# Layer 3's value product in three float32r passes over the key tiles, with its result turned through DRAM

## The chip, the cores and the metric

The kernel runs on one core of one Trainium2 chip. The metric is device time in microseconds of one execution. A run's time is a little longer than the span that the profile covers, which goes from the first to the last instruction of the core.

## What is computed

Input `x` has 32 batches of 512 tokens with 128 features; `adj` is one 512 × 512 matrix that all batches share. Four layers follow one another, each of the form `x = x + layer(relu(layernorm(x)), adj)`. The change is in the last one:

```python
# layer 3, h = relu(layernorm(x))
Q = x @ q
K = x @ k
A = jnp.einsum('bnd,bmd->bnm', Q, K)
A = A / jnp.sqrt(jnp.float32(input_dimension))
A = jnp.tanh(A / 8.0) * 8.0
A = jnp.exp(A) * A_shape
A = A / jnp.sum(A, axis=-1, keepdims=True)
out = A @ x @ v          # x is h here, A_shape is adj
```

All of it is float32. The kernel computes `A @ (h @ v)`, and calls `h @ v` of a batch `hv`. Layers 0 to 2 are graph layers of other kinds; only the end of layer 2 touches the change.

## The kernel before

**Tiles.** A batch of 512 tokens is held as four blocks of 128 tokens on the partitions (token-major), or with the 128 features on the partitions and the 512 tokens along the row (feature-major). [...] A product can be made in float32, which the profile shows as two instructions for each 128 columns, or as a sum of three products in float32r: both operands are split beforehand into parts called high, low and mid (`three`, and the helpers `moving_parts`, `fixed_parts`, `scaled_parts`, `bank_parts` at L420 to L445), so that the three passes together give the exact product up to a known factor, `UP`.

**Turning.** Token-major h becomes feature-major in two steps (`turn_half`, L1144): VectorE transposes 32 × 32 blocks (L1150), and four writes to a DRAM tile followed by one read (`fetch`, L1159) move the blocks to their places. The tokens then lie in a permuted order, which the reading patterns called `crossed` and `split` undo.

**Layer 3, batch by batch.** For each batch n:

- `key_parts(n)` splits feature-major h into three key parts: ScalarE (L437), VectorE (L438), GpSimd (L439).
- `queries(n)` multiplies the parts with the product of q and k (L1271), and splits the result, the query, by ScalarE and VectorE (L443 to L445).
- `mapped(n)` makes hv: a float32 product of the four 128-token blocks of h with v (`projected`, L458), eight instructions in all, copied by VectorE from PSUM into an SBUF tile with a 129th column of ones (L1282, L1283). That column later gives the row sums.
- `scores(n)` makes the 512 × 512 scores in four tiles of three passes (L1298). ScalarE takes tanh (L1299) and exp (L1291); then the mask is multiplied in, by VectorE for tiles 0 and 2 and by GpSimd for 1 and 3 (L1293).
- `attended(n)` multiplies with hv in float32 (L1320), and VectorE divides by the row sum and adds to x (L1322, L1324). The batch is then written out.

**Order.** The order on TensorE, VectorE, ScalarE and GpSimd is that of the source, written out by hand in `layers_2_and_3` (from L1340); DMAs that are wrapped in `keep_in_program_order` keep theirs in SP's queue. The loop of layer 3 is shifted by stages: turn n does `queries(n+1)`, `key_parts(n+2)`, `scores(n)`, `attended(n-1)` and `mapped(n+1)`, with the turning of later batches between. The last two batches are written out apart. The loop of layer 2 ahead of it does per turn `opened(n+1)` (L1212, L1215), `summed(n)` (L1235), `weighed_by_phi(n+1)` (p_z, L458) and `updated(n-1)` (p_l, L458); its last turns already make the key parts of batches 0 and 1 and the query of batch 0.

**Buffers that matter.** All products take one of eight PSUM banks in rotation. `small_tile` gives one of 13 buffers (query parts, hv, and in layer 2 the parts of h, features and hidden rows). `matrix_tile` gives one of three larger ones; in layer 3 the mask holds one of them.

Of the kernel before, what the change touches and what calls it, by code (L numbers as in the profile page):

```python
# [9 lines left out]
F32 = mybir.dt.float32  # L10
F32R = mybir.dt.float32r
# [3 lines left out]
OP = mybir.AluOpType  # L15
AX = mybir.AxisListType

P = 128
QR = 32
NQR = P // QR  # L20
# [3 lines left out]
LOW = 4096.0  # L24
DOWN = 1.0 - 1.0 / 8192.0
UP = 1.0 + 1.0 / 4096.0
# [3 lines left out]
def kernel(  # L30
# [37 lines left out]
    nc = tc.nc  # L68
    B, N, D = x.shape
    NT = N // P  # L70
# [11 lines left out]
    bounce = ctx.enter_context(tc.tile_pool(name="bounce", bufs=4, space=bass.MemoryType.DRAM))  # L82

    def bank(name):
        return psum.tile([P, 512], F32, tag="bank", name=name)
# [11 lines left out]
    def matrix_tile(name, dtype=F32):  # L97
        return const.tile([P, NT, N], dtype, tag="matrix", name=name, bufs=3)
# [4 lines left out]
    def small_tile(name, dtype=F32):  # L103
        return after.tile([P, N], dtype, tag="small", name=name, bufs=13)
# [72 lines left out]
    vw = load_rows(v_w, "vw")[:, 0, :]  # L177
# [244 lines left out]
    def moving_parts(x, high, low, mid):  # L422

        nc.scalar.activation(high, x, AF.Copy, scale=DOWN)  # L424
        nc.gpsimd.tensor_sub(low, x, high.bitcast(F32))  # L425
        nc.vector.scalar_tensor_tensor(mid, x, 1.0 / UP, high.bitcast(F32), OP.mult, OP.subtract)
# [26 lines left out]
    def projected(name, *terms):  # L453

        p = bank(name)
        for t in range(NT):
            for i, (hT, w) in enumerate(terms):
                nc.tensor.matmul(p[:, blk(t)], hT(t), w, start=(i == 0),  # L458
                                 stop=(i == len(terms) - 1))
        return tiles(p)  # L460
# [78 lines left out]
    for t in range(NT):  # L539
        for s in range(t + 1):  # L540
            nc.tensor.matmul(pi[:, t : t + 1], upto[:, s, blk(t)], rch[:, s : s + 1],
                             start=(s == 0), stop=(s == t))

    p = bank("p_qk_t")
# [27 lines left out]
    parts = []  # L572
# [9 lines left out]
    hT = {q: feature_major(f"hT0_{q}") for q in range(4)}  # L582
# [5 lines left out]
    for t in range(NT):  # L588
# [4 lines left out]
        for j in range(NT):  # L593
            nc.tensor.matmul(pg[j // 2][:, j % 2, :], m[:, t, blk(j)], of_row[:, t, :],
                             start=(t == 0 and j % 2 == 0), stop=(t == NT - 1), skip_group_check=True)
    pb = bank("p_known")[:, : 2 * NK].rearrange("p (k e) -> p k e", e=2)
    for kk in range(NK):
        for t in range(NT):
            nc.tensor.matmul(pb[:, kk, :], of_row[:, t, blk(kk)], known[:, t, :],
                             start=(t == 0), stop=(t == NT - 1))  # L600
# [565 lines left out]
    def hT_of(layer, n):  # L1166
        return hTs[layer, n // 2][:, :, n % 2, :]
# [3 lines left out]
    keys, query, hvs, exs = {}, {}, {}, {}  # L1171
# [47 lines left out]
    def weighed_by_phi(n):  # L1219

        if n >= B:
            return
        p = projected(f"p_z_{n}", (columns(features[n]), w2[:, 0, :])).rearrange("p t f -> p (t f)")
        if n:
            z = matrix_tile(f"z_{n}", F32R)
            weighed_features[n] = [z[:, i] for i in range(3)]
        else:
            weighed_features[n] = three(f"z_{n}")
        bank_parts(p, *weighed_features[n])
# [8 lines left out]
    def relu_of(n):  # L1238

        hidden[n] = small_tile(f"hidden_{n}")  # L1240
        nc.scalar.activation(crossed(hidden[n]), split(sums2[n]), AF.Relu, bias=phi1b, scale=UP)
# [15 lines left out]
    def key_parts(n):  # L1257

        if n >= B:
            return  # L1260
        both = wide_tile(f"key_{n}", F32R)
        keys[n] = [both[:, i].rearrange("p (t n) -> p t n", t=NQR) for i in range(3)]
        scaled_parts(hT_of(3, n), *keys[n])

    def queries(n):

        if n >= B:
            return
        p = bank(f"p_query_{n}")
        for i in range(3):  # L1270
            nc.tensor.matmul(p, qk_parts[i], keys[n][i], start=(i == 0), stop=(i == 2))  # L1271
        query[n] = three(f"query_{n}")
        bank_parts(p, *query[n])

    def mapped(n):

        if n >= B:
            return
        hT = hT_of(3, n)
        p = projected(f"p_hv_{n}", (lambda t: hT[:, t, :], vw))  # L1280
        hv = hvs[n] = after.tile([P, NT, D + 1], F32, tag="small", name=f"hv_{n}", bufs=13)
        nc.vector.memset(hv[:, :, D : D + 1], 1.0)  # L1282
        nc.vector.tensor_copy(hv[:, :, :D], p)  # L1283

    def scores(n):

        ex = exs[n] = wide_tile(f"ex_{n}")
        mask = adjTx[0]

        def exponential(t):  # L1290
            nc.scalar.activation(ex[:, t, :], ex[:, t, :], AF.Exp, scale=8.0)  # L1291
            eng = nc.gpsimd if t % 2 else nc.vector
            eng.tensor_mul(split(ex[:, t, :]), split(ex[:, t, :]), crossed(mask[:, t, :]))  # L1293

        for t in range(NT):
            p = bank(f"p_score_{n}_{t}")
            for i in range(3):
                nc.tensor.matmul(p, keys[n][i][:, t, :], query[n][i], start=(i == 0), stop=(i == 2))  # L1298
            nc.scalar.activation(crossed(ex[:, t, :]), split(p), AF.Tanh, scale=UP / (8.0 * math.sqrt(D)))  # L1299
            if t:  # L1300
                exponential(t - 1)
        exponential(NT - 1)
# [25 lines left out]
        if width > 1 and end == NT:  # L1328
            tc.keep_in_program_order(nc.sync.dma_start(out_r, x))

    qk_parts = []

    def weights_of_3():

        parts = small_tile("qk_parts", F32R)[:, : 3 * D].rearrange("p (i f) -> p i f", f=D)
        qk_parts.extend(parts[:, i, :] for i in range(3))
        moving_parts(qk, *qk_parts)
        nc.gpsimd.tensor_scalar(vw, vw, 1.0 / LOW, 1.0, OP.mult, OP.mult)

    def layers_2_and_3():  # L1340


        later, ready, rooted = iter(range(B)), [(2, 6)], []
        late_stats = [stats_steps(q) for q in range(NQ - 4, NQ)]
        stats_of_3 = [stats_steps(q, low=True) for q in range(NQ - 1)]

        def ahead_of_3():
            m = next(later, B)
            if m < B:
                chunk(3, m)  # L1350
                ready.append((3, m))

        def turn_ready(now):
            for layer, m in now:
                turn_half(layer, m)

        mask_of = adjT_d.rearrange("(a b c) w -> b a c w", a=NT, c=QR)
        for n in range(B):
            opened(n + 1)
            turn_ready(ready)  # L1360
            ready = []
            for steps in rooted:
                next(steps)
            if 7 <= n < B - 1:
                ahead_of_3()
            if n + 7 < B:
                chunk(2, n + 7)
                ready.append((2, n + 7))
            split_hT(n + 2)
            for steps in rooted:  # L1370
                go(steps)
            rooted = []
            halves = [(stats_of_3, n - 2)] if 2 <= n else []
            halves += [(late_stats, n)] if n < 8 else []
            for of_pair, m in halves:
                go(of_pair[m // 2], 2)
                if m % 2:
                    rooted.append(of_pair[m // 2])
            summed(n)
            biased(n)  # L1380
            relu_of(n)
            if n == B - 1:
                queries(0)
            weighed_by_phi(n + 1)
            updated(n - 1)
            if n == 0:
                fetch(2, 2)
            elif n % 2 and n + 5 < B:
                fetch(2, n // 2 + 3)
            if n == 12:  # L1390
                weights_of_3()
            if n == 20:
                adjTx.append(matrix_tile("adjTx"))
            if n >= 20 and n % 2 and n < 28:
                i = (n - 20) // 2
                tc.keep_in_program_order(nc.sync.dma_start(adjTx[0][:, i, :], mask_of[i]))
            if n in (26, 28, 30):
                fetch(3, (n - 26) // 2)
            if n in (29, 30):
                key_parts(n - 29)  # L1400
        for steps in rooted:
            go(steps)
        last_stats = low_stats(NQ - 1)
        key_parts(2)
        mapped(0)
        updated(B - 1)
        for n in range(B):
            last = n == B - 1
            queries(n + 1)
            if n:  # L1410
                key_parts(n + 2)
            if n in (4, 6, 8):
                go(last_stats, 1)
            if last:
                attended(n - 2, NT // 2)
            else:
                scores(n)
                if n == B - 2:
                    attended(n - 1, 0, NT // 2)
                    mapped(n + 1)  # L1420
                    scores(n + 1)
                    continue
            attended(n - 1)
            mapped(n + 1)
            if n % 2:
                turn_ready(ready)
                ready = []
            elif n:
                ahead_of_3()
            if n % 2 == 0:  # L1430
                fetch(3, n // 2 + 3)
        attended(B - 1, width=1)
# [109 lines left out]
```

## Time and profile before

| what | value |
|---|---|
| runs | 889.18, 890.08, 890.42 us; median 890.08 |
| the profiled execution | 888.95 us |
| its span | 887.2 us, 15609 instructions |
| TensorE clock granted | 1.00 |
| layer 3's loop | from about 630 us to the end |
| products p_hv (L458) | 256 instructions, first 628.8, last 871.6 us |
| copies to hv (L1283), VectorE | 32 of 684 ns |
| masks (L1293) | VectorE 64 of 1268 ns, GpSimd 64 of 1559 ns |
| HBM | read 44.11 MB, written 40.89 MB |

Durations are of one instruction. A TensorE product starts before the one ahead of it has ended, so its duration (275 ns for p_hv) is longer than its distance from the next; the chain of work counts the distance. PE is TensorE, PEld its loading of weights, DVE VectorE, ACT ScalarE, POOL GpSimd, SPq the queue of SyncE, which issues nearly all DMAs.

### The profile page before, as it was taken

What the parts mean: (1) busy time and instruction counts of PE and PEld (TensorE: products, weight loads), DVE (VectorE), ACT (ScalarE), POOL (GpSimd) and SP (SyncE); (2) the same over time, 40 slices, a digit from 0 to 9 for tenths busy, and PEclk for the clock granted to TensorE, in tenths of its full rate; (3) what the DMA queues carried; (4) which work ended last, traced back from release to release, by engine and by line L of the source; (5) the groups of instructions that cost most, each with busy time, mean ns of one, the idle gap of its engine ahead of it and who ended that gap; (6) DMA issues with size and microseconds to landing.
All of it is one profiled execution on the core that took longest, in us unless ns stands there. A gap on an engine that the chain in (4) does not pass through costs nothing.

```text
span 887.2 us, 15609 instructions
## 1 busy us (share of the span) xinstructions
PE 879.2 (99%) x5369; PEld 774.3 (87%) x5369; DVE 712.5 (80%) x1476; ACT 569.8 (64%) x1288; POOL 598.8 (67%) x535
## 2 busy tenths in 40 slices
PE   8999999999999999999999999999999999999998
PEld 4899999988888888888888888888899999999997
DVE  7888887568787887888688887787799888887775
ACT  5874454456656556556666888876677677766664
POOL 5876999976767877767586665663565666556652
PEclk9999999999999999999999999999999999999999
DMA  9166554032313122222242444555113223322111
GB/s 266 44 170 167 166 144 114 29 96 71 117 51 96 48 72 72 59 85 72 72 143 72 117 125 139 146 157 149 48 60 100 71 69 107 85 82 62 48 37 48
DMA packets 83919, 86.02 MB, mean 97 GB/s; under 512 B 6912, under 2 KB 74624, under 8 KB 83840
## 3 DMA queue, kind: packets, MB, share of 16 engines
q1 hardware_dynamic: 83552, 84.50, 33.6%
q8 instruction: 42, 0.69, 0.3%
q10 hardware_dynamic: 288, 0.52, 0.2%
q14 instruction: 37, 0.30, 0.1%
HBM read 44.11 MB, written 40.89 MB: 96 GB/s over the span
## 4 chain that ended last, share of the span: by engine, by line
PE 95%; POOL 2%; ACT 1%; issue 1%; DMA 1%; DVE 0%; SPq 0%; POOLq 0%; ACTq 0%
PE p_av L1320 13%; PE p_l L1031 10%; PE p_hidden L1235 10%; PE p_score L1298 10%; PE p_x1T L409 9%; PE p_w L1010 5%; PE p_l_c L397 4%; PE p_hv L458 3%; PE p_z L458 3%; PE p_l_a L397 3%; PE p_l L458 3%; PE p_l_d L397 3%; PE p_g L458 3%; PE p_w L1012 3%; PE p_query L1271 3%; PE p_feat L1212 3%
## 5 line engine op out<-in xcount | busy, mean ns | idle before, releaser
L1320 PEld LDWEIGHTS p_av<-hv,ex 128*128 128x128 f32 x1024 | 119.3, 191 | 2.8
L439 POOL TENSOR_TENSOR key<-key 128x512 fp32r<-128x512 f32 x32 | 49.5, 1547 | 104.4 <-DVE key L438 53.5
L1320 PE MATMUL p_av<-hv,ex 128*128 128x129 f32 x1024 | 119.5, 274 | 0.0
L289 ACT ACTIVATE h<-x,sh,rs 128x128 f32<-128x128 f32 x256 | 102.1, 483 | 12.0 <-DVE sh L259 11.0
L1293 DVE TENSOR_TENSOR ex<-ex,adjTx 128x512 f32<-128x512 f32 x64 | 81.2, 1268 | 33.6 <-ACT ex L1291 31.9
L1293 POOL TENSOR_TENSOR ex<-ex,adjTx 128x512 f32<-128x512 f32 x64 | 98.6, 1559 | 10.4 <-ACT ex L1291 6.2
L1141 ACT ACTIVATE h<-x,sh,rs 128x128 f32<-128x128 f32 x256 | 102.9, 486 | 0.0
L247 DVE BATCH_NORM_STATS2 bn<-x 128x6 f32<-128x256 f32 x244 | 87.3, 418 | 0.0
L425 POOL TENSOR_TENSOR low_h<-h,high_h 128x512 fp32r<-128x512 f32 x32 | 54.5, 1706 | 46.1 <-PE p_w L1012 28.0
L1291 ACT ACTIVATE ex<-ex 128x512 f32<-128x512 f32 x128 | 78.8, 650 | 0.0
L1299 ACT ACTIVATE ex<-p_score 128x512 f32<-128x512 f32 x128 | 73.8, 603 | 1.4 <-PE p_score L1298 1.1
L443 ACT ACTIVATE high_query<-p_query 128x512 fp32r<-128x512 f32 x32 | 19.2, 599 | 70.0 <-PE p_query L1271 70.0
L1199 POOL TENSOR_SCALAR high_hT<-hT 128x512 fp32r<-128x512 f32 x32 | 20.1, 629 | 56.5 <-PE p_hidden L1215 31.8
L1255 POOL TENSOR_TENSOR x<-x,phi2b 128x256 f32<-128x256 f32 x64 | 56.6, 905 | 0.0
L425 POOL TENSOR_TENSOR low_hs<-hs,high_hs 128x512 fp32r<-128x512 f32 x32 | 44.4, 1398 | 13.0 <-ACT high_hs L424 12.7
L411 ACT COPY x1T<-p_x1T 128x512 f32<-128x512 f32 x32 | 18.7, 585 | 52.2 <-PE p_x1T L409 52.2
L1298 PE MATMUL p_score<-high_query,key 128*128 128x512 f32 x128 | 50.5, 395 | 0.0
L1298 PE MATMUL p_score<-low_query,key 128*128 128x512 f32 x128 | 50.5, 394 | 0.0
L1298 PE MATMUL p_score<-mid_query,key 128*128 128x512 f32 x128 | 50.4, 394 | 0.0
L256 ACT ACTIVATE sd<-bn,eps 128x8 f32<-128x8 f32 x46 | 13.9, 303 | 55.0 <-DVE bn L247 50.9
L1012 PE MATMUL p_w<-th,x1T 128*128 128x128 f32 x256 | 49.0, 273 | 0.0
L444 DVE SCALAR_TENSOR_TENSOR z<-p_z,z 128x512 fp32r<-128x512 f32 x31 | 21.4, 691 | 32.7 <-ACT z L443 32.6
(253 smaller groups left out, 2631.4 us busy)
## 6 DMA issues: line engine op xcount, KB each, us to landing
d<-hb SPq DMA_DIRECT2D x128, 128.0 KB, 2.4
hT<-d SPq DMA_DIRECT2D x32, 512.0 KB, 3.8
d_hT<-hb_hT SPq DMA_DIRECT2D x112, 128.0 KB, 2.4
hT<-d_hT SPq DMA_DIRECT2D x28, 512.0 KB, 3.4
x<-in_x_dram SPq DMA_DIRECT2D x32, 256.0 KB, 4.7
out_dram<-x SPq DMA_DIRECT2D x31, 256.0 KB, 2.3
adjT_d<-adj_squares SPq DMA_DIRECT2D x4, 256.0 KB, 4.6
adj_crossed<-in_adj_dram SPq DMA_DIRECT2D x4, 256.0 KB
```

Of the source, the lines that this page charges most:

```text
L247: nc.vector.bn_stats(st[:, k].rearrange("p e s -> p (e s)"), xt[q][:, b, t : t + 2, :].rearrange("p t f -> p f t"))
L289: nc.scalar.activation(h[:, b, t, :], xt[q][:, b, t, :], AF.Relu, bias=shift[q][:, i : i + 1], scale=scale[q][:, i : i + 1])
L397: nc.tensor.matmul(p[:, i * 2 * D : (i + 1) * 2 * D], a[:, k, blk(i)], b[:, k], start=(first and i == 0 and k == 0), stop=(k == 1), skip_g ...
L409: nc.tensor.matmul(p, right[part][:, blk(t)], left[part][:, t, :], start=(t == 0 and part == 0), stop=(t == NT - 1 and part == 2))
L425: nc.gpsimd.tensor_sub(low, x, high.bitcast(F32))
L458: nc.tensor.matmul(p[:, blk(t)], hT(t), w, start=(i == 0), stop=(i == len(terms) - 1))
L1031: nc.tensor.matmul(p, adj_parts[part][:, t, blk(i)], w[r][part][:, t, :], start=(part == 0 and t == 0), stop=(part == 2 and t == NT - 1))
L1141: nc.scalar.activation(h[:, t, :], xt[q][:, b, t, :], AF.Relu, bias=shift[q][:, i : i + 1], scale=scale[q][:, i : i + 1])
L1235: nc.tensor.matmul(sums2[n], weighed_features[n][i][:, blk(t)], sq[i][:, t, :], start=False, stop=(i == 2 and t == NT - 1), skip_group_che ...
L1293: eng.tensor_mul(split(ex[:, t, :]), split(ex[:, t, :]), crossed(mask[:, t, :]))
L1298: nc.tensor.matmul(p, keys[n][i][:, t, :], query[n][i], start=(i == 0), stop=(i == 2))
L1320: nc.tensor.matmul(po[:, i, : D + 1], ex[:, t, blk(i0 + i)], hv[:, t, :], start=(t == 0), stop=(t == NT - 1))
```

## The change

`mapped(n)` no longer multiplies token blocks of h with v. It multiplies v, split once into three float32r parts (`vw_parts`), with the three key parts of the batch, which are feature-major h already split: three passes of 512 columns. The result lies feature-major in PSUM. VectorE transposes its 32 × 32 blocks into a small tile, four DMAs write them to a DRAM tile, and one reads them back into a matrix tile (`hvt`). A new function, `straight_values(n)`, has GpSimd copy that tile in straight order into the hv tile, beside a column of `1.0 / UP` that GpSimd sets.

The places in the order change as well. `mapped(0)` and `mapped(1)` are issued in the last two turns of layer 2's loop; `mapped(n+1)` stands ahead of the scores of batch n, right behind the next query; `straight_values(n)` stands behind the scores of n, and for batch 0 ahead of them. `weights_of_3` splits v in place of scaling it by `1.0 / LOW`.

```diff
+    values, turned_values = {}, {}
+
     def mapped(n):
 
         if n >= B:
             return
-        hT = hT_of(3, n)
-        p = projected(f"p_hv_{n}", (lambda t: hT[:, t, :], vw))
+        p = bank(f"p_hv_{n}")
+        for i in range(3):
+            nc.tensor.matmul(p, vw_parts[i], keys[n][i], start=(i == 0), stop=(i == 2))
+        hb = small_tile(f"hvb_{n}").rearrange("p (j t r) -> p j t r", j=NQR, t=NT)
+        nc.vector.transpose(hb.rearrange("p j t r -> p t j r"), p.rearrange("p (t j c) -> p t j c", t=NT, c=QR))
+        d = bounce.tile([NQR, QR, NQR, P], F32, tag="dv", name=f"dv_{n}", bufs=4)
+        for i in range(NQR):
+            tc.keep_in_program_order(
+                nc.sync.dma_start(d[:, :, i, :].rearrange("j c e -> c j e"),
+                                  hb[i * QR : (i + 1) * QR].rearrange("c j t r -> c j (t r)")))
+        raw = turned_values[n] = matrix_tile(f"hvt_{n}")[:, 0]
+        tc.keep_in_program_order(
+            nc.sync.dma_start(raw, d.rearrange("j c i e -> (j c) (i e)")))
+
+    def straight_values(n):
+
+        if n >= B:
+            return
         hv = hvs[n] = after.tile([P, NT, D + 1], F32, tag="small", name=f"hv_{n}", bufs=13)
-        nc.vector.memset(hv[:, :, D : D + 1], 1.0)
-        nc.vector.tensor_copy(hv[:, :, :D], p)
+        nc.gpsimd.memset(hv[:, :, D : D + 1], 1.0 / UP)
+        nc.gpsimd.tensor_copy(hv[:, :, :D].rearrange("p t (i r) -> p t i r", r=QR),
+                              turned_values[n].rearrange("p (i t r) -> p t i r", i=NQR, t=NT))
...
-    qk_parts = []
+    qk_parts, vw_parts = [], []
...
         moving_parts(qk, *qk_parts)
-        nc.gpsimd.tensor_scalar(vw, vw, 1.0 / LOW, 1.0, OP.mult, OP.mult)
+        parts = small_tile("vw_parts", F32R)[:, : 3 * D].rearrange("p (i f) -> p i f", f=D)
+        vw_parts.extend(parts[:, i, :] for i in range(3))
+        moving_parts(vw, *vw_parts)
...
             relu_of(n)
+            if n == B - 2:
+                mapped(0)
             if n == B - 1:
                 queries(0)
+                mapped(1)
             weighed_by_phi(n + 1)
...
         key_parts(2)
-        mapped(0)
         updated(B - 1)
         for n in range(B):
             last = n == B - 1
             queries(n + 1)
             if n:
+                mapped(n + 1)
                 key_parts(n + 2)
...
             else:
+                if n == 0:
+                    straight_values(0)
                 scores(n)
+                if n:
+                    straight_values(n)
                 if n == B - 2:
                     attended(n - 1, 0, NT // 2)
-                    mapped(n + 1)
                     scores(n + 1)
+                    straight_values(n + 1)
                     continue
             attended(n - 1)
-            mapped(n + 1)
```

## The prediction, made before the result was known

> **What bounds the kernel now.** I read the page's busy shares first, then the chain that ended last, then a table of busy time by stage, then the order of time inside layer 3. The page says TensorE is busy for 99% of the span, and the chain is 95% TensorE:
>
> ```profile
> PE 879.2 (99%) x5369; PEld 774.3 (87%) x5369; DVE 712.5 (80%) x1476; ACT 569.8 (64%) x1288; POOL 598.8 (67%) x535
> ...
> PE 95%; POOL 2%; ACT 1%; issue 1%; DMA 1%; DVE 0%; SPq 0%; POOLq 0%; ACTq 0%
> ```
>
> An average says nothing of one stage, so here are two stretches of layer 3 (window, us, then busy us and instructions by engine):
>
> ```profile
> 660.00:700.00 40.00, 40.00 (x278) 36.65 (x277) 36.53 (x73) 30.48 (x63) 23.82 (x18) 1.00 0.25 74
> 820.00:870.00 50.00, 50.00 (x346) 45.76 (x345) 38.50 (x81) 32.98 (x66) 28.33 (x18) 1.00 0.15 46
> ```
>
> TensorE never idles in either; asked for the waits of TensorE between 640 and 870 us, the trace lists none. VectorE is second, 36.53 of 40 us at worst. The chain's pieces (start, duration, what) give one turn of layer 3's loop:
>
> ```profile
> 642.40 0.89 PE p_hv L458 x8
> 643.30 0.69 PE p_query L1271 x3
> 643.99 2.78 PE p_score L1298 x12
> 646.77 3.57 PE p_av L1320 x32
> 650.34 0.89 PE p_hv L458 x8
> ```
>
> One turn is 650.34 − 642.40 = 7.94 us, all TensorE. p_hv costs 0.89 us in eight instructions, a three-pass product of 512 columns (p_query) 0.69 to 0.70. So what the change takes off TensorE comes off the end, unless something else becomes late.
>
> [...] an fp32 product of 128 columns costs 0.89 / 4 = 0.22 us, as much as one pass of 512 columns (2.79 / 12 = 0.23). [...] L1293 on VectorE takes 0.69 us with GpSimd idle and 1.67 beside it; L1324, which reads PSUM, stays at 0.35 to 0.36 beside it:
>
> ```profile
> 742.11 0.69 DVE L1293 TENSOR_TENSOR ex<-ex,adjTx 128x512 f32<-128x512 f32 x1
> 744.05 1.67 DVE L1293 TENSOR_TENSOR ex<-ex,adjTx 128x512 f32<-128x512 f32 x1 [1.25 <-ACT ex L1291]
> 743.90 2.95 POOL L1293 TENSOR_TENSOR ex<-ex,adjTx 128x512 f32<-128x512 f32 x2
> ```
>
> [...]
>
> **The change part by part.** Rows used:
>
> ```profile
> L1283 DVE COPY hv<-p_hv 128x512 f32<-128x512 f32 x32 | 21.9, 684 | 0.1
> L1150 DVE STREAM_TRANSPOSE hb<-h 128x512 f32<-128x512 f32 x26 | 17.7, 697 | 0.0
> L984 POOL COPY hs<-hT 128x512 f32<-128x512 f32 x32 | 20.1, 658 | 3.7 <-DMA hT<-d_hT 3.6
> ```
>
> *TensorE.* Removed: 32 times eight instructions, each 0.89 us, 28.5 us. Added: 32 times three passes of 512 columns over the same key tiles that p_query reads, 0.70 us each, 22.4. At instruction spacing, 8 × 0.1115 = 0.892 against 3 × 0.2325 = 0.698, so 0.194 us a batch, **6.2 us in all**. The first query after the fp32 products shows no extra cost (0.69), so no switch is priced. All of it lies on the path.
>
> *VectorE.* Removed: the 0.684 us copy and a 0.062 us memset that lay under it. Added: a transpose read from PSUM, which no row shows. The copy from PSUM gives a lower bound of 0.68, [...]; I take 0.70. Net about +0.02 us a batch [...], nothing on the path. Its worst stretch holds 36.53 / 40 × 7.95 = 7.26 us a turn, against a new turn of 7.95 − 0.19 = 7.76; 0.48 us are left. The transpose moves from the end of a turn to behind the query parts. Queued behind it: key low (L438), the masks and the p_av evictions. In turns without other transposes VectorE had filled a gap with the copy, so key low and what follows comes some 0.6 us later. The masked scores are used one turn later, with over 2 us to spare; p_av's banks are reused a full turn later. Cost taken: none.
>
> *GpSimd.* Added a turn: a copy as L984's, 0.66 us (up to 1.6, the slowest one-input instruction of this size, the L675 one), and a memset of about 0.1. It had 137.41 us of work in 230, that is 4.75 of 7.95; now 5.5 of 7.76. The copy stands last, behind both masks. It falls beside VectorE's evictions, which read PSUM [...]. hv is then there about 9.2 us after the start of its turn, or 9.8 with the later key; p_av wants it at 7.76 + 0.70 + 0.70 + 2.79 = 11.9. Slack 2 to 2.8 us. In turn 1, where the table load had made ScalarE late, GpSimd's masks end at 645.1 us, the copy at 645.9, and p_av of batch 1 comes at about 646.7: 0.8 us. At the end, masks of batch 31 end 3.97 us after its scores, hv at 4.85, p_av at 5.35: 0.5 us. Cost taken: none, at most 1 us in those two places.
>
> *DMAs, SP's queue.* Added a turn: four writes (1.78 us to issue, as L1156's four) and a read (0.44). The writes land 2.4 us after issue, the read 3.8. From the transpose's end, 1.8 + 2.4 + 0.4 + 3.8 = 8.4 us, so hv is in SBUF about 12 us after the turn's start, and GpSimd reads it at 7.76 + 8.3 = 16. Slack 4 us. The read blocks SP until the writes have landed; behind it wait the output of the batch before (nobody waits for it), the writes of layer 3's other turns and the fetch (used four turns later, some 31 us). SP had about 1.5 us of issuing a turn, now 3.7 of 7.76. The read's buffer is one of two left beside the mask; it is free once GpSimd copied the batch two before, early in the same turn. No cost.
>
> *The entry to layer 3.* mapped(0) goes in ahead of p_z of batch 31, at 622.3 us; its last key part is done by GpSimd at 621.93. mapped(1) follows queries(0), near 628.7; its last key part ends near 628.9 once pushed, and is read by the third pass at 629.2. Cost 0, at most 0.3. The 0.3 us gap ahead of p_hidden of batch 31 stays (both neighbours stay). GpSimd's copy of batch 0 stands ahead of all its masks: written from 624, landed at about 632.4, done by 633.2, first mask at 636.2, three microseconds to spare; were it later, masks and then p_av of batch 0 would wait.
>
> *Weights and buffers.* Splitting vw adds 0.3 us on ScalarE and VectorE and 0.2 on GpSimd once, under layer 2's TensorE work. One more small tile stays for good: of 13, nine are left in layer 2 for five new tiles a turn; the tightest reuse, of hidden, still comes about 1.5 us after its last read. No cost.
>
> *Sum.* −6.2 on a span of 887.2 and an execution of 888.95: 882.75. The median of the runs is 1.13 us above that execution, so 890.08 − 6.2 = **883.9**.
>
> **The rivals.**
> *Forecast*, 883.9 (chance 0.62), 882.8 to 885.2: all 32 savings count.
> *VectorE takes over where it is fullest* (0.17): GpSimd's copy meets a two-input VectorE instruction and blocks it once a turn, 0.66 us. Then a turn from 640 to 740 us costs 7.26 + 0.02 + 0.66 = 7.94 and gains nothing; 12.6 turns × 0.19 = 2.4 us are lost: 886.3. For it: the 1.67 us row. Against it: the place, beside PSUM readers.
> *No gain* (0.08): stalls of 0.19 us a turn eat it, 890.
> *hv comes late, slower* (0.13): the way of hv through DRAM takes so long that GpSimd waits for the read, and p_av for GpSimd. With the later key, GpSimd asks for the read 4.6 us after it lands and p_av for the copy 2.1 us after it is done, so 6.7 us of lateness are free; beyond, each turn pays the excess, 30 times over. From 6.2 / 30 = 0.21 us of excess the kernel is slower, from 0.27 measurably. With the slowest issue of four writes seen (2.97 us in place of 1.78, at 627.5 us) and both landings twice as long (+2.4, +3.8) it is 7.4 us late: 0.7 × 30 = 21 us, 905. For it: the writes' runs are 128 elements, half of L1156's. Against it: the transfer engines are 24% busy from 640 to 870 us.
> That the change does not save TensorE time I exclude: p_query has the same shape and operands.
>
> **How the numbers follow.** Faster by over 0.2% (1.8 us, about what a measurement can tell from no change): 0.62 + 0.17 = 0.79. Within: 0.08. Slower: 0.13. Range: below, the full gain and the runs' own spread (889.18 is 0.9 under the median), 882.8; above, to 888.0, past the VectorE case [...] and half a microsecond for the two thin places.
>
> **What would show it.** Right: p_hv pieces of 0.70 us and a turn of 7.76 us in the chain, TensorE without waits from 640 us on, VectorE over 93% busy from 660 to 700. [...] GpSimd's copy near 0.66. Wrong: p_av released by the GpSimd copy (hv late), p_av or p_score released by VectorE (it is the bound), or GpSimd waiting for the read ahead of its copy.

## The result and the profile after

| | median, us | runs, us |
|---|---|---|
| before | 889.85 | 889.18, 890.08, 890.42, 889.62 |
| changed | 883.44 | 883.48, 883.37, 883.73, 883.40 |

The ratio is 0.9929, with a 95% interval of 0.9912 to 0.9946: the changed kernel is faster by 0.7%. Its profiled execution took 883.48 us with a span of 881.7, where before it was 888.95 and 887.2. So the spans differ by 5.5 us and the medians by 6.4; the runs before spread wider, and their median lies 0.9 us above the profiled execution.

The page still shows a kernel bound by TensorE, with fewer instructions and 6.6 us less of them:

```profile
PE 872.6 (99%) x5209; PEld 763.3 (87%) x5209; DVE 713.2 (81%) x1445; ACT 576.5 (65%) x1289; POOL 618.0 (70%) x599
...
PE 93%; POOL 3%; ACT 2%; DVE 1%; issue 1%; DMA 0%; POOLq 0%; ACTq 0%
```

The chain has more of GpSimd and ScalarE in it than before (3% and 2%, in place of 2% and 1%): a first hint that something waits. In layer 3 the chain now leaves TensorE twice: from 632.7 to 639.8 us, where it runs through ScalarE and GpSimd for batch 0, and from 691.4 to 702.1 us, where it runs through VectorE and GpSimd. One ordinary turn in the chain's pieces (start, duration, what):

```profile
650.78 0.70 PE p_query L1271 x3
651.48 0.69 PE p_hv L1283 x3
652.18 2.76 PE p_score L1317 x12
654.94 3.57 PE p_av L1339 x32
658.51 0.69 PE p_query L1271 x3
```

p_hv is now 0.69 us in three instructions where it was 0.89 in eight, and the turn is 658.51 − 650.78 = 7.73 us where it was 7.94. The two stretches of the loop by engine (window, us, then busy us and instructions of PE, PEld, DVE, ACT, POOL; clock, DMA share, GB/s):

```profile
660.00:700.00 40.00, 40.00 (x257) 35.80 (x256) 35.14 (x70) 32.34 (x64) 26.80 (x28) 1.00 0.52 145
700.00:740.00 40.00, 39.39 (x254) 34.99 (x253) 35.64 (x64) 30.23 (x60) 28.08 (x28) 1.00 0.56 153
```

TensorE is full in the first and lacks 0.61 us in the second. From 660 to 700 us VectorE got no fuller (35.14 where it was 36.53), and the transfer engines are busy twice as much (0.52 where it was 0.25). Asked who waited for whom from 690 to 704 us, the trace names the missing piece (us in total, times, longest):

```profile
PEld p_av L1339 <- POOL hv L1301: 1.1, 1, 1.1
PE p_av L1339 <- POOL hv L1301: 0.6, 1, 0.6
```

Once, for batch 8, p_av waits for GpSimd's copy of hv. The order of time there shows why (first TensorE, then GpSimd):

```profile
702.06 3.84 PE L1339 MATMUL p_av<-hv,ex 128*128 128x129 f32 x32 [0.61 <-POOL hv L1301]
694.00 1.59 POOL L439 TENSOR_TENSOR key<-key 128x512 fp32r<-128x512 f32 x1 [2.83 <-DVE key L438]
695.68 0.57 POOL L275 TENSOR_SCALAR sd<-bn 128x8 f32<-128x8 f32 x1
696.32 0.24 POOL L276 TENSOR_SCALAR sh<-bn 128x8 f32<-128x8 f32 x1
696.53 1.67 POOL L277 TENSOR_TENSOR rs<-sd,minus_half 128x8 f32<-128x8 f32 x1
698.28 0.21 POOL L278 TENSOR_TENSOR sh<-sh,rs 128x8 f32<-128x8 f32 x1
698.45 2.54 POOL L1312 TENSOR_TENSOR ex<-ex,adjTx 128x512 f32<-128x512 f32 x2
700.93 0.11 POOL L1300 MEMSET hv<- 128x4 f32 x1
700.97 1.04 POOL L1301 COPY hv<-hvt 128x512 f32<-128x512 f32 x1
```

Between the key part and the masks GpSimd makes the last layernorm statistics of layer 3 (`low_stats`, 2.8 us from 695.68 to 698.45). Before the change they stood in the same place, but only the masks stood behind them, and those had time: they end at 701.62 us, and p_av of batch 8 starts at 702.27.

```profile
697.17 1.66 POOL L277 TENSOR_TENSOR rs<-sd,minus_half 128x8 f32<-128x8 f32 x1
698.91 0.20 POOL L278 TENSOR_TENSOR sh<-sh,rs 128x8 f32<-128x8 f32 x1
699.07 2.55 POOL L1293 TENSOR_TENSOR ex<-ex,adjTx 128x512 f32<-128x512 f32 x2
702.35 1.28 POOL L439 TENSOR_TENSOR key<-key 128x512 fp32r<-128x512 f32 x1 [0.72 <-DVE key L438]
```

Now hv stands behind the masks. In the changed kernel the last score product starts at 701.05 and p_av at 702.06, 1.01 us later where 0.23 is usual: 0.78 us of TensorE lost. The 32 products of that p_av take another 0.11 us longer than usual (3.60 us in place of 3.49), so the turn loses about 0.9 us: 8.65 us where its neighbours take 7.73 and 7.74.

The copy itself adds to its lateness. It takes 1.04 us, where the other 31 take 0.60 to 0.62. Being late, it falls beside two VectorE instructions that have two inputs in SBUF, and these take 1.08 and 1.09 us in place of 0.65 and 0.68 to 0.69:

```profile
700.46 1.08 DVE L438 SCALAR_TENSOR_TENSOR key<-key,hT 128x512 fp32r<-128x512 f32 x1
701.46 1.09 DVE L1312 TENSOR_TENSOR ex<-ex,adjTx 128x512 f32<-128x512 f32 x1
```

So what the prediction feared in every turn happens in this one.

### The profile page after: what moved, and what is told of

It is laid out like the page before. It is cut to its first block, busy times and chain, and to the rows that moved or that the text cites. A ratio compares the mean times of both kernels' runs of the same rounds, so it can differ in the third digit from the quotient of the medians.

```text
span 881.7 us, 15654 instructions
## 1 busy us (share of the span) xinstructions
PE 872.6 (99%) x5209; PEld 763.3 (87%) x5209; DVE 713.2 (81%) x1445; ACT 576.5 (65%) x1289; POOL 618.0 (70%) x599
## 4 chain that ended last, share of the span: by engine, by line
PE 93%; POOL 3%; ACT 2%; DVE 1%; issue 1%; DMA 0%; POOLq 0%; ACTq 0%
PE p_av L1339 13%; PE p_l L1031 10%; PE p_hidden L1235 10%; PE p_score L1317 9%; PE p_x1T L409 9%; PE p_w L1010 5%; PE p_l_c L397 5%; PE p_l L458 3%; PE p_z L458 3%; PE p_l_a L397 3%; PE p_l_d L397 3%; PE p_g L458 3%; PE p_w L1012 3%; PE p_feat L1212 3%; PE p_hidden L1215 3%; PE p_query L1271 2%
## 5 line engine op out<-in xcount | busy, mean ns | idle before, releaser
L289 ACT ACTIVATE h<-x,sh,rs 128x128 f32<-128x128 f32 x256 | 102.2, 483 | 11.9 <-DVE sh L259 11.0
L1312 DVE TENSOR_TENSOR ex<-ex,adjTx 128x512 f32<-128x512 f32 x64 | 80.5, 1260 | 31.0 <-ACT ex L1310 29.2
L1312 POOL TENSOR_TENSOR ex<-ex,adjTx 128x512 f32<-128x512 f32 x64 | 99.6, 1573 | 6.9 <-issue 3.5
L1318 ACT ACTIVATE ex<-p_score 128x512 f32<-128x512 f32 x128 | 76.3, 598 | 11.5 <-PE p_score L1317 4.7
L1150 DVE STREAM_TRANSPOSE hb<-h 128x512 f32<-128x512 f32 x64 | 43.6, 698 | 2.8 <-DMA d<-hb 2.6
```

What stands on the lines that cost most here:

```text
L289: nc.scalar.activation(h[:, b, t, :], xt[q][:, b, t, :], AF.Relu, bias=shift[q][:, i : i + 1], scale=scale[q][:, i : i + 1])
```

## Experiments

**The passes alone.** In the kernel before:

```diff
-        hT = hT_of(3, n)
-        p = projected(f"p_hv_{n}", (lambda t: hT[:, t, :], vw))
+        p = bank(f"p_hv_{n}")
+        for i in range(3):
+            nc.tensor.matmul(p, vw_parts[i], keys[n][i], start=(i == 0), stop=(i == 2))
...
-        nc.vector.tensor_copy(hv[:, :, :D], p)
+        nc.vector.tensor_copy(hv[:, :, :D], tiles(p))
...
```

Further on, v is split into its three parts as in the change.

> The kernel before with the three float32r passes in place of the eight float32 instructions, in the old place, and copied by VectorE as before; the turn through DRAM and GpSimd's copy are left out, so hv has its blocks in a wrong layout. Theory (the whole gain is TensorE's, 0.194 us for each of 32 batches): 6.2 us less than before, about 883.6, and no wait of TensorE in layer 3's turns; the gap ahead of p_hidden of batch 31 as before. Rival (the gain comes from the new places in the order, or the passes cost more on TensorE than the query's): within 2 us of before.

Measured: 882.79 us against 889.62 of before, ratio 0.9922 (0.9909 to 0.9936). The last product of TensorE starts at 877.25 us, before at 883.44: 6.19 us earlier. The end of layer 2 came 0.2 us later in this trace: counted from the last p_feat there, the gain is 6.41 us. TensorE lists no wait of its own in the loop, and the turn in the chain has the same pieces as the changed kernel's, in the old order:

```profile
649.91 0.70 PE p_hv L1281 x3
650.61 0.69 PE p_query L1271 x3
651.29 2.79 PE p_score L1299 x12
654.08 3.58 PE p_av L1321 x32
657.66 0.69 PE p_hv L1281 x3
```

An ordinary turn takes 7.75 us on average, before 7.95: 0.20 us each. So the gain is TensorE's and comes from the passes. The gap ahead of p_hidden of batch 31 was expected to stay and is gone, though the order there is that of before.

**The turn alone.** In the changed kernel:

```diff
-        p = bank(f"p_hv_{n}")
-        for i in range(3):
-            nc.tensor.matmul(p, vw_parts[i], keys[n][i], start=(i == 0), stop=(i == 2))
+        hT = hT_of(3, n)
+        p = projected(f"p_hv_{n}", (lambda t: hT[:, t, :], vw)).rearrange("p t f -> p (t f)")
```

> The changed kernel with hv made by the eight float32 instructions again, in the new place; transposes, writes, reads and GpSimd's copy stay (the product that is turned is token-major, so hv is wrong). Theory (all that the turn adds is hidden): as before within 1 us, 889 to 891, with at most a wait of p_av of 0.4 to 0.8 us in the turn where GpSimd also makes the last statistics. Rival (the turn costs time in every turn of the loop): 892 or more.

Measured: 889.00 us against 889.62, ratio 0.9995 (0.9987 to 1.0003). With all its transposes, 160 DMAs and 32 GpSimd copies the turn through DRAM costs nothing that shows in the time. In the trace the turn of the statistics loses 0.35 us (8.30 us in place of 7.95), with an 0.48 us distance ahead of p_av in place of 0.23; the gap ahead of p_hidden, which is gone here too, gives 0.3 us back. The loss is smaller than in the changed kernel, as turns longer by 0.2 us give GpSimd more time: its copy starts 3.5 us after that turn's start, in the changed kernel 4.0.

**The old place for the new product.** In the changed kernel:

```diff
-            if n:
-                mapped(n + 1)
+            if n == B - 2:
+                mapped(n + 1)
+            if n:
                 key_parts(n + 2)
...
             attended(n - 1)
+            if 0 < n < B - 2:
+                mapped(n + 1)
```

> The changed kernel with mapped(n+1) back behind attended(n-1) for turns 1 to 29, so that the turn through DRAM begins some 5.7 us later in its turn (2.79 of scores, 3.57 of p_av, less 0.70 of its own). Theory (6.7 us of lateness are free: 4.6 ahead of GpSimd's copy and 2.1 behind it): as the changed kernel within 1 us, 883 to 884.5, GpSimd now waiting for the read in some turns. Rival (the slack is thinner than 5.7 us by x): p_av waits for GpSimd's copy in nearly every turn, 29 times x; with 1 us, 912.

Measured: 884.11 us, ratio to before 0.9942 (0.9929 to 0.9956). The 5.7 us are nearly all free. GpSimd now asks for the read 2.7 to 3.9 us after it was issued in most turns, where it was 8 to 10, and the read lands after 2.7; in three turns it has to wait:

```profile
POOL hv L1301 <- DMA hvt<-dv: 2.4, 3, 1.3
```

p_av still waits in two places only: for the masks of batch 0 (that turn takes 8.88 us, in the changed kernel 8.12) and for hv of batch 8, behind the statistics. The early place buys 0.7 us, nearly all of it in the turn of batch 0, and a margin; it is not what makes the turn through DRAM possible.

**The changed kernel again,** on the same chip as these three:

> The changed kernel as it is, for the same chip: 6.4 us less than before, about 883.4, with the same one wait of p_av for GpSimd's copy of 0.8 us near 702 us.

Measured: 883.45 us, ratio 0.9929 (0.9916 to 0.9941), with the same distance of 1.02 us ahead of p_av, which starts at 701.89. So the passes alone are 0.7 us faster than the whole change, which is about this one wait.

**The statistics behind the copy.** In the changed kernel:

```diff
-            if n in (4, 6, 8):
+            if n in (4, 6):
                 go(last_stats, 1)
...
                 if n:
                     straight_values(n)
+                if n == 8:
+                    go(last_stats, 1)
```

> The changed kernel with the last step of the last statistics (four GpSimd instructions, 2.8 us from 695.7 us on) moved behind GpSimd's copy of hv in the same turn. Theory (p_av waits 0.8 us at 702 us because these stand ahead of the masks and the copy): the wait is gone, 0.8 us less than the changed kernel, about 882.6. Rival (the wait has another cause, such as the read landing late): the same time, 883.4, with the wait still there.

Measured: 882.49 us against 889.78, ratio 0.9922 (0.9909 to 0.9934). The wait at 702 us is gone from the trace: the turn that took 8.65 us takes 7.77, and the copy, which now stands ahead of the statistics, takes 0.62 us and is done 2.1 us before p_av wants it:

```profile
699.68 0.62 POOL L1301 COPY hv<-hvt 128x512 f32<-128x512 f32 x1
700.38 0.20 POOL L275 TENSOR_SCALAR sd<-bn 128x8 f32<-128x8 f32 x1
```

From the last p_feat of layer 2 to the last product this is 0.91 us less than the changed kernel, the whole loss of that turn. The cause of the one long wait is shown. The execution that was profiled is the slowest of the five, 883.75 us; its clock was at half for 3.4 us at the start of the kernel, far from the change (see the last section).

**The table loaded early as well:**

```diff
         key_parts(2)
+        nc.scalar.activation(stats.tile([P, 1], F32, name="tanh_table", bufs=1), eps, AF.Tanh)
         updated(B - 1)
```

> As the kernel with the statistics moved, and with a one-column Tanh on ScalarE behind key_parts(2), whose result nobody reads, so that the 1.28 us table load falls into ScalarE's idle time ahead of the scores of batch 0. Theory (the table load makes the masks of batch 0 late, which p_av waits 0.23 us for at 639.8 us): 0.2 us less again, about 882.4. Rival (the wait there is GpSimd's own): no difference from the kernel with the statistics moved.

Measured: 883.54 us, runs from 882.15 to 884.18, ratio 0.9926 (0.9914 to 0.9939). In the profiled execution the wait of p_av of batch 0 is gone (that turn takes 7.66 us, before the edit 8.11), but the time decided nothing. A second measurement, on another chip:

> The kernel with the statistics moved and the table loaded early, a second time, because its five runs lay between 882.15 and 884.18. Theory (nothing is left that waits; the spread is of the runs): TensorE without a wait from 600 us on again, and a median of 882.2 to 882.8, some 1 us under the changed kernel. Rival (the added instruction makes some executions slower): again half of the runs above 883.4.

Measured: 882.09 us, runs from 881.93 to 882.14, ratio 0.9916 (0.9902 to 0.9929). The trace lists no wait of TensorE from 600 us to the end. In both profiled executions the stretch from the last p_feat to the last product is 1.36 and 1.35 us shorter than in the changed kernel. Seven of the ten runs show it (881.93 to 882.47 us, against 883.44); the other three took 883.54 to 884.18, and why stays open: no trace shows them.

**GpSimd's copy three times over:**

```diff
-        nc.gpsimd.tensor_copy(hv[:, :, :D].rearrange("p t (i r) -> p t i r", r=QR),
-                              turned_values[n].rearrange("p (i t r) -> p t i r", i=NQR, t=NT))
+        for _ in range(3):
+            nc.gpsimd.tensor_copy(hv[:, :, :D].rearrange("p t (i r) -> p t i r", r=QR),
+                                  turned_values[n].rearrange("p (i t r) -> p t i r", i=NQR, t=NT))
```

> The changed kernel with GpSimd's copy of hv made three times over, so 1.2 us more of GpSimd a turn, all ahead of hv. Theory (2.1 to 2.8 us of slack between the copy and p_av): nothing in ordinary turns, 1.2 us more at 702 us and 0.5 to 0.8 us in turn 1 and at the end, so 885.5 to 886.5. Rival (GpSimd's copy and VectorE's instructions with two SBUF inputs block one another, and VectorE is nearly the bound): up to 0.6 us in each of 30 turns, 890 or more.

Measured: 890.10 us, ratio 1.0006 (0.9998 to 1.0015). The time is the rival's, and I had it wrong; but the rival's reason, a loss in each turn, does not hold either. Ordinary turns take 7.72 to 7.79 us as before. The loss sits in four places: batch 1 and the last batch (p_av waits 1.3 and 1.2 us), the turn of the statistics, and the time right behind it. The first line is of TensorE in order of time, the rest are stretches by engine:

```profile
705.62 5.48 PE L1340 MATMUL p_av<-hv,ex 128*128 128x129 f32 x32 [3.01 <-POOL hv L1302]
```

```profile
702.00:706.00 4.00, 0.99 (x5) 0.55 (x4) 2.63 (x3) 2.89 (x6) 3.88 (x6) 0.97 0.49 144
706.00:709.50 3.50, 3.50 (x20) 3.50 (x20) 0.14 (x1) 0.00 (x0) 3.50 (x5) 0.54 0.26 75
709.50:713.00 3.50, 3.50 (x24) 3.15 (x23) 2.46 (x8) 1.12 (x2) 1.57 (x3) 1.00 0.01 4
```

TensorE waits 3.0 us, since the three copies stand behind the statistics in GpSimd's queue, and since they fall beside VectorE's instructions with two inputs in SBUF: they take 3.23 us, in an ordinary turn 1.96.

```profile
702.34 3.23 POOL L1302 COPY hv<-hvt 128x512 f32<-128x512 f32 x3
709.23 1.96 POOL L1302 COPY hv<-hvt 128x512 f32<-128x512 f32 x3
```

Then TensorE's clock falls to half for some 3.4 us, and the 32 instructions take 5.48 us in place of 3.73: another 1.7 us.

To part the two, the same in the version with both mends:

> GpSimd's copy made three times over, in the kernel with the statistics moved and the table loaded early. Theory (in the kernel with three copies, 3.0 us of idle TensorE at 702 us, from copies and statistics together, and the 3.4 us at half clock behind it made most of the loss): no half clock, no wait at 702 us, about 1 us in turn 1 and 1.1 at the end, so 884 to 885. Rival (the copies take from VectorE in every turn): 888 or more.

Measured: 886.46 us, ratio 0.9965 (0.9953 to 0.9978): neither number. The clock stays full and the 3.0 us wait is gone. In its place p_av waits in the next turn, behind the statistics that were moved there:

```profile
711.77 0.49 PE L1340 MATMUL p_av<-hv,ex 128*128 128x129 f32 x2 [1.24 <-POOL hv L1302]
```

p_av waits 1.4 us there, 1.05 for batch 1 and 1.2 for the last batch, together 3.6 of the 4.4 us between this version and the mended one. Ordinary turns take 7.73 to 7.78 us again. So even three copies cost an ordinary turn nothing; GpSimd's queue has 2.1 to 2.7 us to spare per turn and less in special ones.

**VectorE's transpose twice:**

```diff
-        nc.vector.transpose(hb.rearrange("p j t r -> p t j r"), p.rearrange("p (t j c) -> p t j c", t=NT, c=QR))
+        for _ in range(2):
+            nc.vector.transpose(hb.rearrange("p j t r -> p t j r"), p.rearrange("p (t j c) -> p t j c", t=NT, c=QR))
```

> The changed kernel with VectorE's transpose of each hv made twice (the second writes the same values), 0.7 us more of VectorE a turn. Theory (VectorE has 0.48 us or more to spare in its fullest turns and over 0.8 in the others): 0 to 2 us more, from the first dozen turns, 883.4 to 885.5. Rival (VectorE is the bound already): 0.7 us in each of 30 turns, 900 or more.

Measured: 885.05 us, ratio 0.9949 (0.9935 to 0.9962). Of the 1.6 us over the changed kernel, 1.2 us sit in two turns that wait for GpSimd (8.38 and 9.26 us, in the changed kernel 7.79 and 8.65); those behind them take 7.73 to 7.77. Another 0.7 us of VectorE a turn does not make it the bound.

## Why the prediction was right, step by step

**TensorE, −6.2 us: right.** An ordinary turn got 0.20 us shorter, with the passes alone and in the changed kernel (0.194 predicted), and the experiments leave no other source of the gain. Reading the cost off p_query, the same shape over the same key tiles, was enough: p_hv takes 0.69 to 0.70 us. That the last product with the passes alone comes 6.19 us earlier is partly luck, since 0.2 us lost in layer 2 and 0.2 at batch 0 offset the gap of 0.3 that went.

**The sum: the forecast 883.9, measured 883.44, and so close partly by luck.** From the start of the last p_feat in layer 2 to the start of the last product, the two traces differ by 5.35 us: −6.2 of the passes, −0.3 for a gap that went, +0.9 at the statistics, +0.2 at batch 0. Layer 2 ended 0.2 us later and the end of the kernel is 0.35 shorter, which makes the 5.5 us of the spans. So the profiled execution, forecast at 882.75, took 883.48 us, 0.7 more. The forecast then added 1.13 us for the runs before, whose median lay that far above their profiled execution; the changed kernel's runs hardly spread, and their median lies 0.04 us under their profiled execution. The two errors offset each other. That the medians differ by 6.4 us and the spans by 5.5 is the spread of the runs before.

**GpSimd, "at most 1 us in those two places": right in size (0.9 us), wrong in place.** The slack of ordinary turns was well read: p_av starts 2.05 to 2.69 us after the copy of hv ends (2 to 2.8 predicted), 0.52 for batch 1 (0.8 predicted) and 0.81 at the end (0.5 predicted). The two named places cost nothing. The wait came where I had not looked: I took GpSimd's work as a mean per turn and checked the first and last turn, not the one turn in which the queue has 2.8 us of other work. That was in the trace of before, as L275 to L278. It is the sign of the rival in which hv comes late, p_av released by GpSimd's copy, but by way of GpSimd's queue and once, not by way of DRAM in each turn. "TensorE without waits from 640 us on" failed in this one turn.

**DMAs: right, with terms too large.** I used the landings of 128 and 512 KB (2.4 and 3.8 us) for 64 and 256 KB; the page after has less (KB, us to landing):

```profile
dv<-hvb SPq DMA_DIRECT2D x128, 64.0 KB, 1.9
hvt<-dv SPq DMA_DIRECT2D x32, 256.0 KB, 2.5
```

The read is issued 8 to 10 us ahead of GpSimd's copy in most turns and lands after 2.5, so some 5.5 to 7.5 us are free there, not 4.6. The kernel with the old place used up nearly all of it, at a cost of 0.7 us in time.

**VectorE: right that it is not the bound, wrong on how full it gets.** The transpose from PSUM takes 0.707 us (0.70 taken, at least 0.68 by the copy from PSUM). The upper end of my range, 888.0, held 1.0 us for a slower transpose; that was my estimate, and no row of before showed it. I expected over 93% from 660 to 700 us and got 88%. What fell is the masks, 12.2 us in place of 14.1 for ten: my explanation, that in the new order they meet GpSimd's instructions less, was not tested by itself. The place of GpSimd's copy was read right: 31 of the 32 copies are not slowed (0.60 to 0.62 us), and VectorE's L1343, which reads PSUM, takes 0.34 to 0.35 us with GpSimd at work or not. One row was misread: the 0.69 us of L1293 at 742.11 were not beside an idle GpSimd. GpSimd's key part began 0.13 us later and took 1.70 us, where the fastest take 1.27:

```profile
742.24 1.70 POOL L439 TENSOR_TENSOR key<-key 128x512 fp32r<-128x512 f32 x1 [3.46 <-PE p_score L1298]
```

So there the second to begin was slowed, and the first was not.

**The entry to layer 3: the gap of 0.3 us "stays" was wrong.** It is absent after the change and also with the passes alone, where the order is the old one. Why it was there in the trace of before is open. The wait of p_av of batch 0 (0.23 us) is the table load, 1.28 us on ScalarE ahead of its first tanh, which stands there before the change too: the early Tanh removes the wait.

## What to carry to other kernels

On a bound engine, price a replaced product by a row of the same shape, and count distances between starts, not durations. When a step moves onto another engine's queue, don't judge it by the mean turn: list what else that queue does in each turn, because one odd turn decides. Where two steps share a queue, put the one first that the bound engine needs; here that and an early table load took another 1.35 us out of the trace.

## What the runs showed of the hardware

One wait of TensorE of 3.0 us (3.4 between starts) was followed by about 3.4 us at half clock (the mean from 706 to 709.5 us is 0.54): 32 instructions took 5.48 us in place of 3.73. So this stall cost 1.7 us more than its length, while waits of up to 1.4 us in layer 3 left the clock at 1.00. In the run with the statistics moved the clock is at half from 8.5 to 11.9 us, at the start of the kernel, behind waits of 1.13 and 0.37 us. That execution, with a mean granted clock of 0.998, took 1.3 us more than the median of its five, though its layer 3 has no such stretch. What brings the clock to half these runs do not show.

A transpose of 128 × 512 float32 costs VectorE 0.707 us from PSUM and 0.702 from SBUF (medians), a difference of 0.005 us.

In layer 3 of the changed kernel VectorE's masks (L1312), which read two tiles in SBUF, take 0.68 to 0.69 us where GpSimd is idle as they begin, and up to 1.81 where it is at work. GpSimd's copy goes from 0.61 to 1.04 us in the one turn in which it meets such instructions.
